# Spacing the feed-forward blocks of a macaron layer along a planner's beats

## The chip, the cores and the metric

The kernel runs on one core of a Trainium2 chip (trn2). The metric is device time of one execution in microseconds (us), as the median of three runs. The five engines are called as in the profile: PE (TensorE matmuls; PEld are its weight loads), DVE (VectorE), ACT (ScalarE), POOL (GpSimd) and SP (SyncE, which only issues DMAs here).

## The reference

32 sequences of 256 tokens with 128 features pass through one "macaron" layer: half a feed-forward block, attention, half a feed-forward block.

```python
x = x + 0.5 * ffn(layernorm(x))        # first FFN
x = x + attn(layernorm(x))             # 16 heads of 8, softmax, then a layernorm of (ctx + input)
x = x + 0.5 * ffn(layernorm(x))        # second FFN, same weights

def ffn(x):                            # weights are +1 or -1, drawn as booleans
    h = concat([x, -x])
    h = s0 * (h @ k0);  h = relu(h) * 2     # 512 features
    h = s1 * (h @ k1);  h = relu(h) * 2     # 512
    return s2 * (h @ k2)                    # 128
```

## The kernel before

Two sequences make a unit of 512 tokens; there are 16 units (`NU`). For each unit the kernel does a first FFN (`first`), a normalization and projection for attention (`norm_attn`, `project`), row maxima of the scores (`maxima`), a shift row made from them (`shift`), the softmax weights and their products with the values (`weigh`), the context with its layernorm (`context`), and a second FFN (`second`). Activations that feed a matmul are held as a sum of a high and a low fp16 part, so each 512-column product of an FFN is two passes on PE.

An FFN of a unit is 4 steps of layer 0 and 16 steps of layer 1 (two passes of 128x512 each) and 4 groups of layer 2 (8 passes of 128 columns). After each 128x512 result `relu_split` makes the high part on ACT (L663) and the low part on DVE (L664). The planner may move that work: the low part to POOL, after a full-precision copy on ACT (L666, then L661), or both parts to POOL (L667, then L661). The last sum can go from DVE (L718) to ACT and POOL (L719, L720) in the same way.

`maxima` and `weigh` set the beat. Each of a unit's 16 beats has one score tile for the maxima (`nat`, L825, reduced on DVE at L836 into `nm`) and, 13 beats later (`BW`), one for the weights (`sc`, L895, exponentiated on ACT at L907 into `pt`). Both kinds take the same pool of two PSUM tiles. Products with the values (`cx`, L877) follow each pair of `sc` tiles. There are 256 beats of maxima; the beats of weights end 13 later.

All operations go into a list with an engine, an assumed cost and a *rank*, which is a place on the scale of beats. `_Plan.simulate` runs through that list at build time with the assumed costs, and so decides which instruction is emitted next on each engine: on PE the lowest ranks first, with FFN work (kind "F") used as filling between the beats; on the others the lowest rank that is ready. The order found is fixed; on the chip each engine runs its own queue in that order and waits on semaphores. The constants at the top (`BIAS`, `CAST`, `SKIP`, `RUSH`, `AHEAD` and others) steer this planner and do no work of their own.

A matmul can be emitted in two tilings: dense ("D", L420, one 128x128 weight) or as four column tiles ("C", L423, four of 128x32). Score tiles use row tiles of 32 ("R"). The planner takes for an FFN step the tiling that PE is in.

Where an FFN's work lies along the beats is set by its rank:

```python
first(u):   rank = B0 + P0 * u                 # B0 = -30, P0 = 16.003
second(u):  rank = B1 + max(u * UNIT, P1 * min(u, SLOW) + P2 * max(u - SLOW, 0))
            # UNIT = 16, B1 = 42.462, P1 = 17.354, SLOW = 1, P2 = 16
```

so both kinds follow each other at 16 beats, one of each per unit. `QF` and `QK` say for how many units the normalizations take a quick form, which is done on DVE (L612) in place of POOL (L617, L618).

Of the kernel before, what the change touches and what calls it, by code (L numbers as in the profile page):

```python
# [41 lines left out]
ALU = mybir.AluOpType  # L42
# [7 lines left out]
EPS = 1e-5  # L50
# [4 lines left out]

PT, NXN = 5, 5

QF, QK = 1, 1

QL = 1  # L60

# [1 line left out]


UNIT = 16
B0, BA, BP, BW, BV, B1 = -30, -10.627, -6.547, 13, 4, 42.462

P0, P1, P2, SLOW = 16.003, 17.354, 16, 1

TURN_X, TURN_C = 1.5, 1.5  # L70

WARM = 14

BB = 15.813

RUSH, AHEAD = -0.12, 4.08

SKIP0, SKIP, UNTIL = 10.311, 2.868, 28.215

FAR = 19.64  # L80

HOLD = (0, 0.0, 0.0)

CAST = 1.0

WAIT = 0.057

KIND2 = 'F'

# [2 lines left out]

AFTER, REACH = (0.165, 0.085, 0.11, 0.04, 0.0), (0.053, 0.033, 0.037, 0.08, 0.05)

BIAS = 1.115

BIAS2 = 0.714
PE, DVE, ACT, POOL, SP = range(5)


# [19 lines left out]
class _Plan:  # L120
# [11 lines left out]
    def op(self, eng, cost, emit, r=(), w=(), rank=0.0, kind="D", rows=0, lag=None, alt=None, rush=False):  # L132
        x = _Node()
        x.n, x.eng, x.cost, x.emit, x.rank, x.kind, x.rows = len(self.nodes), eng, cost, emit, rank, kind, rows
        x.lag, x.alt, x.tiling = lag, alt, "D"
        x.then, x.avail, x.start, x.rush = [], 0.0, None, rush
        x.pair = None
        needs = set()
        for k in r:
            if k in self.wrote:  # L140
                needs.add(self.wrote[k])
        for k in w:
            if k in self.wrote:
                needs.add(self.wrote[k])
            needs.update(self.read.pop(k, ()))
        for k in r:
            self.read.setdefault(k, []).append(x)
        for k in w:
            self.wrote[k] = x
        needs.discard(x)  # L150
        x.needs = list(needs)
        for y in x.needs:
            y.then.append(x)
        x.bufs = []
        for k in (*r, *w):
            b = k[0] if isinstance(k, tuple) else k
            if isinstance(b, _Buf) and b not in x.bufs:
                x.bufs.append(b)
                b.left += 1
        self.nodes.append(x)  # L160
        return x
# [228 lines left out]
def tile_macaron(ctx: ExitStack, tc: tile.TileContext, x, Wq, bq, Wk, bk, Wv, bv, gamma, beta, k0, k1, k2, s0, s1, s2, out):  # L390
    nc = tc.nc
    plan = _Plan(tc)
    op = plan.op
# [3 lines left out]
    NU = B // 2  # L397
    TU = 2 * S
    NT = TU // P
# [94 lines left out]
    scale = const.tile([P, 3], F32, name="scale")  # L494
# [5 lines left out]
    def projections():  # L500
# [15 lines left out]
        s = lambda emit, w, rank=-700: op(SP, 0.42, emit, w=w, rank=rank, lag=4.5)  # L516
        v = lambda cost, emit, r, w, rank=B0 + BB: op(DVE, cost, emit, r=r, w=w, rank=rank)
        for i, (W, b) in enumerate(((Wq, bq), (Wk, bk), (Wv, bv))):
# [71 lines left out]
    def normalize(dst, src, tag, n, rank, scale=1.0, quick=False):  # L590

        of = lambda: src[0].t[:, src[1] : src[1] + n]
        srcs = [(src[0], src[1] + t) for t in range(0, n, 2)]
        mv = buf(small, [P, n, 2], F32, f"mv{tag}", 4, f"mv_{tag}")
        ve = buf(small, [P, n], F32, f"ve{tag}", 4, f"ve_{tag}")
        rs = buf(small, [P, n, 1], F32, f"rs{tag}", 4, f"rs_{tag}")
        step = 2 if quick else n
        for a in range(0, n, step):
            part = slice(a, a + step)
            ts = range(a, a + step)  # L600
            for t in ts:
                st = buf(small, [P, 6], F32, f"st{tag}", 4, f"st_{tag}_{t}")
                op(DVE, 0.195, lambda t=t, st=st: nc.vector.bn_stats(st.t, of()[:, t, :]), r=[srcs[t // 2]], w=[st], rank=rank)
                op(DVE, 0.085, lambda t=t, st=st: nc.vector.bn_aggr(mv.t[:, t, :], st.t), r=[st], w=[(mv, t)], rank=rank)
            op(POOL, 0.27, lambda part=part: nc.gpsimd.tensor_scalar(ve.t[:, part], mv.t[:, part, 1], EPS, 1.0 / scale**2, ALU.add, ALU.mult),
               r=[(mv, t) for t in ts], w=[(ve, a)], rank=rank)
            op(POOL, 0.35 + 0.2 * step, lambda part=part: nc.gpsimd.tensor_tensor(rs.t[:, part, 0], ve.t[:, part], nhalf[:, part], ALU.pow),
               r=[(ve, a), "nhalf"], w=[(rs, a)], rank=rank)
        mvs = [(mv, t) for t in range(n)]
        if quick:  # L610
            for t in range(n):
                op(DVE, 0.26, lambda t=t: nc.vector.tensor_scalar(dst.t[:, t, :], of()[:, t, :], mv.t[:, t, 0:1], rs.t[:, t, :], ALU.subtract, ALU.mult),  # L612
                   r=[srcs[t // 2], (rs, t // 2 * 2), (mv, t)], w=[(dst, t)], rank=rank)
        else:
            dsts = [(dst, t) for t in range(n)]
            cost = 0.2 + 0.2 * n
            op(POOL, cost, lambda: nc.gpsimd.tensor_tensor(dst.t, of(), bc(mv.t[:, :, 0:1], D), ALU.subtract), r=[*srcs, *mvs], w=dsts, rank=rank)  # L617
            op(POOL, cost, lambda: nc.gpsimd.tensor_tensor(dst.t, dst.t, bc(rs.t, D), ALU.mult), r=[(rs, 0)], w=dsts, rank=rank)  # L618
# [19 lines left out]
    xs, xns, xTs, nms, cxs = {}, {}, {}, {}, {}  # L638
# [11 lines left out]
    def norm_ffn(key, src, n, rank, quick):  # L650
        name = f"{key[0][-1]}_{key[1]}_{key[-1]}"
        xn = buf(work, [P, n, D], F32, "fxn", 2, f"fxn{name}")
        normalize(xn, src, f"f{key[0][-1]}", n, rank, XS, quick)
        xTs[key] = turned(xn, key[0][-1], name, n, rank)
# [15 lines left out]
    def ffn(key, srcs, n, rank, span):  # L670

        xT = xTs.pop(key)
        w = n * P
        name = f"{key[0][-1]}_{key[1]}_{key[-1]}"

        at = lambda i: rank + span * i / (NF + NF * NF + n)
        LAYER2 = (lambda k: k) if KIND2 == "F" else (lambda k: 2 * (k // 2) + 0.9)
        i = 0
        h1 = [buf(work, [P, NF, w], F16, f"h1{p}", 2, f"h1{p}{name}") for p in "hl"]
        h2 = [buf(work, [P, NF, w], F16, f"h2{p}", 2, f"h2{p}{name}") for p in "hl"]  # L680
        step = 2 * w / 2370
        for m in range(NF):
            ph = psum([P, w], f"p1{name}_{m}")

            def layer0(tiling, m=m, ph=ph):
                for k in range(2):
                    dense(ph.t, w0[:, bass.ts(m, P)], xT.t[:, k, :], tiling, k == 0, k == 1)

            op(PE, step, layer0, r=["w0", *((xT, i, a) for i in range(2) for a in range(0, n, 2))], w=[ph], rank=at(i), kind="F")
            relu_split(*h1, m, ph, w, at(i))  # L690
            i += 1
        for m in range(NF):
            ph = psum([P, w], f"p2{name}_{m}")
            for c in range(NF):

                def layer1(tiling, m=m, c=c, ph=ph):
                    for k in range(2):
                        dense(ph.t, w1[:, c, bass.ts(m, P)], h1[k].t[:, c, :], tiling, c == 0 and k == 0, c == NF - 1 and k == 1)

                op(PE, step, layer1, r=[("w1", c), (h1[0], c), (h1[1], c)], w=[ph], rank=at(i), kind="F")  # L700
                i += 1
            relu_split(*h2, m, ph, w, at(i))
        po = psum([P, n, D], f"p3{name}")
        h2s = [(h, m) for h in h2 for m in range(NF)]
        for t in range(n):

            def layer2(tiling, t=t):
                for c in range(NF):
                    for k in range(2):
                        dense(po.t[:, t, :], h2[k].t[:, c, bass.ts(t, P)], w2[:, c, :], tiling, c == 0 and k == 0, c == NF - 1 and k == 1)  # L710

            op(PE, 0.449, layer2, r=[*h2s, "w2"], w=[po], rank=LAYER2(at(i)), kind=KIND2)
            i += 1
        src, part = srcs
        full = buf(work, [P, w], F32, "full", 2, "full")
        to = lambda: src.t[:, part : part + n]
        dsts = [(src, part + t) for t in range(0, n, 2)]
        op(DVE, 0.08 + w / 870, lambda: nc.vector.scalar_tensor_tensor(to(), po.t, fac, to(), ALU.mult, ALU.add), r=[po, "fac"], w=dsts, rank=at(i),  # L718
           alt=(0.09 + w / 1040, lambda: nc.scalar.activation(full.t.rearrange("p (t d) -> p t d", d=D), po.t, AF.Identity, scale=fac), po, full,  # L719
                0.1 + w / 455, lambda: nc.gpsimd.tensor_tensor(to(), to(), full.t.rearrange("p (t d) -> p t d", d=D), ALU.add)))  # L720
        return dsts

    def norm_first(u):
        norm_ffn(("ffn0", u), (xs[u], 0), NT, (B0 + P0 * u - AHEAD) if u >= QF else B0 - 0.5 + 2 * (u - 1) if u else -950, u < QF)

    def first(u):
        rank = B0 + P0 * u
        ffn(("ffn0", u), (xs[u], 0), NT, rank, P0)

    def second(u, b):  # L730
        n, part = (NT, 0) if b is None else (2, 2 * b)
# [270 lines left out]
```

## Time and profile before

| | us |
|---|---|
| median of 3 runs | 688.27 (687.88 to 688.88) |
| time of the profiled execution | 689.46 |
| its span, first to last instruction | 687.6 |
| PE busy | 659.8 (96%) |
| DVE busy | 581.1 (85%) |
| ACT busy | 543.1 (79%) |
| POOL busy | 497.3 (72%) |
| granted TensorE clock, mean | 0.995 |

Matmuls are pipelined and their ends are modelled, so a busy PE is not a PE at its peak; the distance from the start of one matmul to the start of the next tells what it costs. A line of a table by stretch of time reads: the stretch, its length, then for each engine the busy time with the number of instructions in brackets, then the granted TensorE clock, the share of DMA engines busy and GB/s. A chain of waits reads: start, length, what the end of the kernel was waiting for at that time. An execution in the profile is 1.2 us slower than the median of the runs; differences are made inside the profiled execution and then taken to the median.

### The profile page before, as it was taken

What the parts mean: (1) busy time and instruction counts of PE and PEld (TensorE: products, weight loads), DVE (VectorE), ACT (ScalarE), POOL (GpSimd) and SP (SyncE); (2) the same over time, 40 slices, a digit from 0 to 9 for tenths busy, and PEclk for the clock granted to TensorE, in tenths of its full rate; (3) what the DMA queues carried; (4) which work ended last, traced back from release to release, by engine and by line L of the source; (5) the groups of instructions that cost most, each with busy time, mean ns of one, the idle gap of its engine ahead of it and who ended that gap; (6) DMA issues with size and microseconds to landing.
All of it is one profiled execution on the core that took longest, in us unless ns stands there. A gap on an engine that the chain in (4) does not pass through costs nothing.

```text
span 687.6 us, 28926 instructions
## 1 busy us (share of the span) xinstructions
PE 659.8 (96%) x12596; PEld 344.6 (50%) x12596; DVE 581.1 (85%) x1194; ACT 543.1 (79%) x871; POOL 497.3 (72%) x685
## 2 busy tenths in 40 slices
PE   7998978999999999999999999999999999999996
PEld 4544533545455554555455454555445454544455
DVE  7789887998989798898979889897988888889484
ACT  3546887788889888888978888897889787868953
POOL 6875596688686868768686877868686785865643
PEclk9999998999999999999999999999999999999999
DMA  7222200203011030301102030200203021300000
GB/s 222 76 79 80 64 23 3 83 5 98 5 49 54 3 98 4 100 4 58 46 5 97 3 99 5 76 27 16 86 5 97 4 74 30 96 4 20 5 17 31
DMA packets 33391, 33.59 MB, mean 49 GB/s; under 512 B 4992, under 2 KB 29056, under 8 KB 33264
## 3 DMA queue, kind: packets, MB, share of 16 engines
q1 hardware_dynamic: 31520, 30.89, 14.3%
q8 instruction: 99, 1.62, 1.0%
q10 hardware_dynamic: 1744, 0.85, 0.4%
q14 instruction: 28, 0.23, 0.1%
HBM read 18.58 MB, written 13.14 MB: 46 GB/s over the span
## 4 chain that ended last, share of the span: by engine, by line
PE 82%; DVE 7%; ACT 4%; POOL 3%; DMA 2%; issue 1%; SPq 0%; ACTq 0%; POOLq 0%
PE p_None L423 18%; PE p L423 17%; PE cx L877 16%; PE sc L895 9%; PE p L420 6%; DVE nm L836 4%; PE p_None L420 3%; PE nat L825 3%; ACT pt L907 2%; PE tp L921 2%; PE pq L423 2%; PE pq L420 1%; PE pv L423 1%; PE t L630 1%; PE t_None L630 1%
## 5 line engine op out<-in xcount | busy, mean ns | idle before, releaser
L836 DVE TENSOR_REDUCE nm<-nat 128x4 f32<-128x1024 f32 x256 | 310.5, 1216 | 27.4 <-PE nat L825 22.0
L907 ACT ACTIVATE pt<-sc,esc 128x1024 f32<-128x1024 f32 x256 | 285.2, 1116 | 54.7 <-PE nat L825 45.2
L423 PEld LDWEIGHTS <-w 128*32 128x32 f16 x3976 | 97.4, 96 | 102.4 <-issue 28.9
L877 PE MATMUL cx<-pt,vaug 128*32 128x256 f32 x2048 | 137.2, 385 | 0.0
L895 PE MATMUL sc<-qs,ks 32*128 32x256 f16 x1024 | 103.2, 274 | 6.7 <-ACT pt L907 4.9
L825 PE MATMUL nat<-ks,qs 32*128 32x256 f16 x1024 | 101.7, 274 | 3.9 <-ACT pt L907 1.8
L877 PEld LDWEIGHTS cx<-pt,vaug 128*32 128x32 f32 x2048 | 58.6, 110 | 44.7 <-issue 12.3
L423 PE MATMUL p<-h1h,w 128*32 128x512 f16 x796 | 78.5, 383 | 0.0
L423 PE MATMUL p<-h1l,w 128*32 128x512 f16 x796 | 78.0, 380 | 0.0
L423 PE MATMUL p_None<-h1h_None,w 128*32 128x512 f16 x744 | 73.6, 382 | 0.1
L423 PE MATMUL p_None<-h1l_None,w 128*32 128x512 f16 x744 | 73.0, 379 | 0.0
L895 PEld LDWEIGHTS <-ks 32*128 32x128 f16 x1024 | 31.7, 92 | 75.0 <-issue 70.7
L661 POOL TENSOR_TENSOR h2l_None<-full,h2h_None 128x512 f16<-128x512 f32 x27 | 31.5, 1168 | 27.6 <-ACT full L666 27.3
L661 POOL TENSOR_TENSOR h2l<-full,h2h 128x512 f16<-128x512 f32 (+1 forms) x36 | 40.8, 1134 | 11.5 <-ACT full L666 10.8
L663 ACT ACTIVATE h1h<-p 128x512 f16<-128x512 f32 (+1 forms) x68 | 37.3, 577 | 13.6 <-PE p L420 9.0
L825 PEld LDWEIGHTS <-qs 32*128 32x128 f16 x1024 | 31.3, 92 | 29.7 <-issue 28.7
L663 ACT ACTIVATE h2h<-p 128x512 f16<-128x512 f32 (+1 forms) x56 | 32.3, 576 | 15.7 <-PE p L420 11.8
L664 DVE SCALAR_TENSOR_TENSOR h2l_None<-p_None,h2h_None 128x512 f16<-128x512 f32 x33 | 22.7, 687 | 25.7 <-ACT h2h_None L663 25.6
L420 PEld LDWEIGHTS <-w 128*128 128x128 f16 x326 | 30.1, 98 | 28.5 <-issue 10.5
L664 DVE SCALAR_TENSOR_TENSOR h1l<-p,h1h 128x512 f16<-128x512 f32 (+1 forms) x61 | 39.4, 663 | 1.1 <-ACT h1h L663 0.8
L663 ACT ACTIVATE h2h_None<-p_None 128x512 f16<-128x512 f32 x56 | 33.4, 596 | 6.0 <-PE p_None L420 4.9
L423 PE MATMUL p_None<-xT_None,w 128*32 128x512 f16 x480 | 35.4, 380 | 0.0
(163 smaller groups left out, 1471.7 us busy)
## 6 DMA issues: line engine op xcount, KB each, us to landing
dr<-qkhl SPq DMA_DIRECT2D x32, 256.0 KB, 2.0
qs<-dr SPq DMA_DIRECT2D x48, 128.0 KB, 3.3
ks<-dr SPq DMA_DIRECT2D x48, 128.0 KB, 2.6
out_dram<-x SPq DMA_DIRECT2D x15, 256.0 KB, 3.0
x<-in_L_attn_x_dram SPq DMA_DIRECT2D x14, 256.0 KB, 6.1
dm<-mr SPq DMA_DIRECT2D x32, 16.0 KB, 2.5
qs<-dm SPq DMA_DIRECT2D x32, 16.0 KB
qs<-nought SPq DMA_DIRECT2D x13, 32.0 KB
```

The lines of the kernel that those rows point to most:

```text
L420: nc.tensor.matmul(to, w, of, start=start, stop=stop)
L423: nc.tensor.matmul(to[32 * r : 32 * r + 32], w[:, 32 * r : 32 * r + 32], of, start=start, stop=stop)
L630: nc.tensor.transpose(pt.t[:, bass.ts(t, P)], xn.t[:, t, :], ident)
L661: return lambda: nc.gpsimd.tensor_tensor(lo.t[:, m, :], of.t, hi.t[:, m, :], ALU.subtract)
L663: h = op(ACT, 0.09 + w / 1280, lambda: nc.scalar.activation(hi.t[:, m, :], ps.t, AF.Relu), r=[ps], w=[(hi, m)], rank=rank)
L664: l = op(DVE, 0.08 + w / 985, lambda: nc.vector.scalar_tensor_tensor(lo.t[:, m, :], ps.t, 0.0, hi.t[:, m, :], ALU.max, ALU.subtract), r=[p ...
L825: nc.tensor.matmul(nat.t[:, ii, qc, :], Q[32 * r : 32 * r + 32, g, b * S + qc * P : b * S + qc * P + P], K[32 * r : 32 * r + 32, g, b * S ...
L836: op(DVE, 1.141, lambda g=g, pr=pr, nat=nat: nc.vector.tensor_reduce(nm.t[:, :, 2 * pr : 2 * pr + 2, g].rearrange("p q i -> p i q"), nat.t ...
L877: nc.tensor.matmul(cx.t[32 * r : 32 * r + 32, g // 2, :], V[:, 2 * b + kc, 4 * (g // 2) + r, 16 * (g % 2) : 16 * (g % 2) + 32], pts[g, r / ...
L895: nc.tensor.matmul(sc.t[:, ii, kc, :], K[32 * r : 32 * r + 32, g, b * S + kc * P : b * S + kc * P + P], Q[32 * r : 32 * r + 32, g, b * S : ...
L907: op(ACT, 1.012, lambda pt=pt, sc=sc: nc.scalar.activation(pt.t, sc.t, AF.Exp, scale=esc), r=[sc, "esc"], w=[pt], rank=rank - RUSH, rush=True)
L921: nc.tensor.transpose(tp.t[:, qc, 8 * c : 8 * c + 8, :].rearrange("p h n -> p (h n)"), cxT.t[:, c, bass.ts(qc, P)], ident)
```

## The change

First FFNs are no longer 16 beats apart. The new function `place0` puts those of units 0 to 6 12 beats apart and the later ones 18.67 apart, so that the last one keeps its place (beat 210). Second FFNs are 16.95 beats apart up to unit 10 and 13.42 apart after it, but never before beat `B1 + 16 u`. The quick normalizations cover more units at the start, and the planner's other constants get other values, among them the assumed cost of a cast on POOL (`CAST`, 1.0 to 0.62). No operation of the layer is added or removed.

```diff
-QF, QK = 1, 1
+QF, QK = 3, 2
-B0, BA, BP, BW, BV, B1 = -30, -10.627, -6.547, 13, 4, 42.462
-P0, P1, P2, SLOW = 16.003, 17.354, 16, 1
-TURN_X, TURN_C = 1.5, 1.5
+B0, BA, BP, BW, BV, B1 = -30, -11.429, -5.976, 13, 4, 44.465
+P1, P2, SLOW = 16.954, 13.418, 10
+EARLY, COUNT, OVER = 12, 6, 0
+TURN_X, TURN_C = 0.3, 1.5
-BB = 15.813
-RUSH, AHEAD = -0.12, 4.08
-SKIP0, SKIP, UNTIL = 10.311, 2.868, 28.215
+BB = 10.463
+RUSH, AHEAD = 0.144, 4.667
+SKIP0, SKIP, UNTIL = 7.606, 3.049, 23.783
-CAST = 1.0
-WAIT = 0.057
+CAST = 0.62
+WAIT = 0.125
-BIAS = 1.115
-BIAS2 = 0.714
+BIAS = 1.03
+BIAS2 = 0.765
...
-            op(POOL, 0.27, lambda part=part: nc.gpsimd.tensor_scalar(ve.t[:, part], ...
+            op(POOL, 0.275, lambda part=part: nc.gpsimd.tensor_scalar(ve.t[:, part], ...
...
+    def place0(u):
+        rest = ((NU - 1) * UNIT + OVER - EARLY * COUNT) / (NU - 1 - COUNT)
+        return B0 + EARLY * min(u, COUNT) + rest * max(u - COUNT, 0)
+
     def norm_first(u):
-        norm_ffn(("ffn0", u), (xs[u], 0), NT, (B0 + P0 * u - AHEAD) if u >= QF else B0 - 0.5 + 2 * (u - 1) if u else -950, u < QF)
+        norm_ffn(("ffn0", u), (xs[u], 0), NT, place0(u) - AHEAD if u >= QF else B0 - 0.5 + 2 * (u - 1) if u else -950, u < QF)
     def first(u):
-        rank = B0 + P0 * u
-        ffn(("ffn0", u), (xs[u], 0), NT, rank, P0)
+        ffn(("ffn0", u), (xs[u], 0), NT, place0(u), min(UNIT, place0(u + 1) - place0(u)))
```

More of the change, by code (lines that the diff above doesn't have):

```diff
@@ L604, in normalize @@
                 op(DVE, 0.085, lambda t=t, st=st: nc.vector.bn_aggr(mv.t[:, t, :], st.t), r=[st], w=[(mv, t)], rank=rank)
-            op(POOL, 0.27, lambda part=part: nc.gpsimd.tensor_scalar(ve.t[:, part], mv.t[:, part, 1], EPS, 1.0 / scale**2, ALU.add, ALU.mult),
+            op(POOL, 0.275, lambda part=part: nc.gpsimd.tensor_scalar(ve.t[:, part], mv.t[:, part, 1], EPS, 1.0 / scale**2, ALU.add, ALU.mult),
                r=[(mv, t) for t in ts], w=[(ve, a)], rank=rank)
```

## The prediction

> **What bounds the kernel now.** I read the page's slices first, then the time and the beats in six stretches (a beat is one `nat` tile of four matmuls), then the chain of waits in the middle and near the end, then PE's timeline for what a matmul costs.
>
> ```profile
> PE   7998978999999999999999999999999999999996
> PEclk9999998999999999999999999999999999999999
> ```
>
> PE has holes in the first ten slices and in the last; one slice early on has a lower clock. By stretch:
>
> ```profile
> core 0: us, PE busy (x) PEld busy (x) DVE busy (x) ACT busy (x) POOL busy (x), PEclk, DMA share, GB/s
> 0.00:43.15 43.15, 36.60 (x230) 21.41 (x231) 32.62 (x111) 21.34 (x48) 32.20 (x51) 1.00 0.50 149
> 43.15:66.90 23.75, 21.26 (x431) 10.19 (x431) 23.30 (x34) 13.59 (x26) 14.26 (x17) 1.00 0.19 59
> 66.90:155.70 88.80, 81.68 (x1517) 40.22 (x1520) 78.00 (x154) 70.59 (x106) 66.19 (x92) 0.96 0.12 35
> 155.70:574.20 418.50, 418.19 (x8672) 217.88 (x8671) 363.96 (x729) 356.67 (x566) 316.29 (x425) 1.00 0.15 47
> 574.20:638.80 64.60, 60.24 (x1152) 29.61 (x1144) 56.95 (x100) 51.24 (x73) 45.90 (x67) 1.00 0.11 33
> 638.80:687.60 48.80, 41.87 (x612) 25.27 (x608) 26.28 (x69) 29.62 (x53) 22.42 (x36) 0.99 0.06 19
> ```
>
> The cuts are at beats 0, 16, 56, 224 and 256: the same stretches asked for `nat` alone hold 0, 64, 162, 672, 128 and 0 matmuls (162 for 160 since a cut fell inside a tile). A beat takes 88.80/40 = 2.22 us, then 418.50/168 = 2.49, then 64.60/32 = 2.02. In the middle PE has no hole, and the chain shows the same step of PE every unit:
>
> ```profile
> 248.98 1.29 PE p_None L423 x24
> 288.65 1.29 PE p_None L423 x24
> 328.33 1.29 PE p_None L423 x24
> ```
>
> 39.67 us a unit: there PE is the bound. Near the end a beat is cheaper in PE work, and the chain leaves PE:
>
> ```profile
> 612.61 1.11 ACT pt L907
> 613.72 0.50 ACT h2h_None L663
> 614.24 0.69 DVE h2l_None L664
> 614.93 1.14 DVE nm L836
> 616.12 0.26 PE nat L825
> 616.61 1.12 ACT pt L907
> ```
>
> Two beats here take 4.0 us: `pt`, a ReLU split queued behind it on ACT, its low part on DVE, the maxima behind that, then the next score tiles. This alternation over the two shared PSUM tiles, not PE, keeps such beats at 2 us.
>
> What PE work costs, from starts in the middle:
>
> ```profile
> 245.44 0.28 PE L895 MATMUL sc<-qs,ks 32*128 32x256 f16 x1
> 245.76 0.62 PE L423 MATMUL p_None<-xT_None,w 128*32 128x512 f16 x8
> 246.21 0.39 PE L423 MATMUL p<-h1h,w 128*32 128x512 f16 x4
> 246.42 0.39 PE L423 MATMUL p<-h1l,w 128*32 128x512 f16 x4
> 246.64 0.61 PE L423 MATMUL p_None<-xT_None,w 128*32 128x512 f16 x8
> ```
>
> A pass of 512 columns is 0.216 us (246.42 to 246.64), dense or in column tiles alike. A score pair with the change to row tiles is 0.32 us (245.44 to 245.76), of which 0.11 is the change of tiling: the same 0.11 stands before row tiles after column tiles (a group of `pv`, 12 passes of 0.056 us, starts at 242.05 and the scores after it at 242.84, not 242.72). So an FFN is 40 x 0.216 + 32 x 0.056 = 10.4 us of PE.
>
> **The change, part by part.** I took the order in which the instructions of both kernels stand on PE and gave each its duration (512 columns 0.216, 128 columns 0.056, `cx` of 8 matmuls 0.87, score pair 0.22, transpose 0.11, change of tiling 0.11). PE work in us, cut at the same beats:
>
> - before beat 0: 33.5 before, 38.7 after
> - beats 0 to 16: 20.0, 23.6
> - 16 to 56: 75.9, 82.5
> - 56 to 224: 414.9, 393.1
> - 224 to 256: 56.7, 63.0
> - the rest: 38.6, 40.1
>
> The sums, 639.6 and 641.0, agree but for changes of tiling: 573 before, 584 after, 11 x 0.11 = 1.2 us more. The middle loses 21.8 us; 15.4 go ahead of it (one and a half FFNs) and 7.8 behind it. The gain is what the edges swallow.
>
> *Before beat 0: +4.0.* PE runs with nearly no hole from 12.26 us to the first `nat` at 43.17; its holes there are 0.30, 0.30, 0.55, 0.52 and 0.45, together 2.1 us. Ahead of the first `nat` stand 22 more passes of 512 columns (4.75 us) and one more transpose group (0.44); the projection that feeds the first keys comes later too, behind most of them, so DMA and landing shift along. Filling half the holes leaves 5.2 - 1.1, about 4.0. Bounds 3 and 5.5. The quicker normalizations add 12 L612 instructions of 0.30 us to DVE, which has 10 us free here, and take 3 x 2.1 us of L617 and L618 from POOL.
>
> *Beats 0 to 16: +1.0.* DVE is busy 23.30 of 23.75, so DVE bounds. Its work in these beats grows by 0.5 us in the new order, and PE at 23.6 gets no slack. Bounds 0.5 and 3.
>
> *Beats 16 to 56: +1.2.* PE has 88.8 - 75.9 = 12.9 us over its work; 6.6 are filled. DVE's work stays at 78 us. The beats lengthen where the filling brings a split into the alternation shown, and against that stands the clock:
>
> ```profile
> 100.00:105.00 5.00, 3.39 (x42) 1.24 (x43) 3.50 (x8) 3.07 (x6) 4.52 (x10) 0.83 0.03 8
> 105.00:110.00 5.00, 3.86 (x40) 1.29 (x39) 3.01 (x6) 2.54 (x3) 2.47 (x4) 0.50 0.01 3
> ```
>
> After two slices with PE at 3.4 to 4 of 5 us the granted clock falls to half for some 6.8 us. PE is busy three quarters of that, so it loses 6.8 x 0.5 x 0.77 = 2.6 us at most. The Trainium skill ("TensorE: Matmul & The Clock Gate", Part 1, the warm-up mystery) puts the cold state after at least one idle window of about 3.4 us. The longest hole before the drop here is 1.2 us (at 93.6), so the row shows the fall under thinner PE work than the rule needs. By the rule a denser PE does nothing for the clock and this stretch costs +3.8; by the row the denser beats (14.7 and 14.4 us of work where 10.4 and 12.0 were) keep the clock up and it costs +1.2. I take the row. Bounds -1 and +6.6 (all new work added, none hidden).
>
> *Beats 56 to 224: -18.8.* The measured 418.5 is 3.6 over its work. The new work is 393.1; with the same 3.6 it is 396.7. The old order repeats unit by unit; the new one doesn't, so the other engines' loads shift against PE's. For what that costs the trace has one near row, the end of the repeating part: beats 192 to 224 (`nat` starts at 493.2 and 574.2) took 81.0 us for 79.8 of PE work, 1.2 over, where 32 repeating beats are 0.6 over. That is 0.02 us a beat, or 3 us over 168: 399.7, or 2.38 us a beat. Bounds 396.7 and, at three times that row, 405.7. Other engines allow it: DVE's work in these beats stays about 2.1 us a beat (88%, as 364/418.5 = 87% before), ACT about 2.0. POOL gets 17 more L661 (1.16 us) and 33 more L667 casts (0.61), in return for 6 L720 and the normalizations: +28 us in the whole kernel, from 76% to some 85% here. ACT loses 16 of L666 (0.60 us), DVE 17 of L664 (0.69) and gains 6 of L718 and 12 of L612. None of these is on the path while PE has work; that cover is thinnest for POOL.
>
> The skill's rule against the change: "TensorEngine Tiling (Array Packing)", Tiling Modes, says that a change of tiling mode drains TensorE. The row prices that drain at 0.11 us, and all 11 more are in the sums; priced by the rule alone no figure would follow.
>
> *Beats 224 to 256: +4.0.* PE has 7.9 us over its work and 6.3 are to be filled, 4.0 of them into the first eight beats (15.8 to 19.8 us of work, measured 16.9). Those eight become PE-bound at about 20.0; the other 24 stay on the 2 us alternation (48.6 us for the 47.7 measured). Half an FFN brings four splits of 0.50 + 0.69 = 4.8 us if all are on the chain. Bounds 2 and 6.3.
>
> *The rest: +1.0.* Of the second FFN of unit 13, 26 passes are left after the last `nat`, before 20: 1.3 us, in beats that ACT's exponentials hold (5.87 of 6.20 us busy after 638.8). Behind the last context two passes more: 0.4. Bounds 0 and 2.
>
> SP issues the same transfers in nearly the same order. Loads of x were all issued at the start, and stores follow their second FFN: no cost, with PE work as cover.
>
> Sum: 4.0 + 1.0 + 1.2 - 18.8 + 4.0 + 1.0 = -7.6. The profiled execution took 689.46, so 681.9 for it; the median lies 1.2 under that, so 680.7, rounded to 681.
>
> **The rivals.** *Ragged middle, slower (chance 0.14).* Without the old period a beat of the middle waits for POOL's low parts or for DVE before PE can go on. It decides at 2.38 + 7.6/168 = 2.425 us a beat; beyond, the kernel is slower. For it: beats 16 to 56, also irregular, carry 12.9/40 = 0.32 us of PE idle each, and POOL rises to 85%. Against: there PE had too little filling, and 192 to 224, with enough, lost 1.2/32 = 0.04. At 0.08 over my forecast the kernel takes 681 + 0.08 x 168 = 694.
>
> *The edges swallow little (chance 0.14).* Early and late beats lengthen by all their new work: 5.2 + 3.6 + 6.6 + 6.3 + 1.5 = 23.2 against -18.8: +4.4, 693. For it: DVE at 98% in beats 0 to 16, the alternation near the end. Against: over 12 us of PE idle lie in beats 16 to 56 with the same DVE load. Half of this, 687, is a likelier form, still faster; so a third of this chance ends faster and some of it level.
>
> *The edges swallow nearly all (chance 0.12).* Clock kept, early beats no longer than now, middle at 396.7: 3.0 + 0.5 - 1 - 21.8 + 2 + 0 = -17 at most; half way to that is 676.
>
> That the change doesn't do what it says is excluded: in PE's new order the first FFN of unit 2 is nearly done before the first `nat`, where before it had just begun.
>
> **How the numbers follow.** Forecast 0.60 (681, own range 676 to 686), ragged 0.14, little swallowed 0.14, nearly all 0.12. Faster by over 0.2% (1.4 us, about what a measurement of this kernel can tell from no change): 0.60 + 0.12 + 0.05 (edges by half) + 0.02 (a slightly ragged middle) = 0.79; within 0.2%: 0.03 + 0.02 of the two slower rivals = 0.05; slower: 0.06 + 0.10 = 0.16. The range goes from 675, under which half of "nearly all" lies, to 689.5, above which most of the slower cases lie.
>
> **What would show it.** First `nat` at about 47 us, beat 56 near 162, beat 224 near 562, beat 256 near 630; no clock drop near 105; a middle beat at 2.38 us with PE without holes; late beats at 2.1 us. If a middle beat is over 2.42, or the chain there leaves PE for POOL h1l, h2l or DVE nm, the forecast is wrong in the middle; if beat 56 is past 168, it is wrong in the early beats.

## The result, and the profile after

The changed kernel takes 693.04 us in the median (16 runs, 688.96 to 696.63) where the kernel before takes 688.04 beside it (16 runs, 687.15 to 689.96): ratio 1.0066, 95% interval 1.0049 to 1.0082. It is slower by two thirds of a per cent; the forecast was 681. Its profiled execution took 693.77 us, with a span of 692.0 (before: 689.46 and 687.6).

The slices of the page of the changed kernel, in the same columns as before:

```profile
PE   7899999999999999999999999999999999989997
PEclk9999999999999999999999999999999999999999
```

The holes of slices 4, 6 and 7 are gone, as the change says. But slice 2 is emptier than before (8 for 9), slice 36 has a hole now, and the whole is longer, so one has to look by stretch. The same stretches as in the prediction, cut at beats 0, 16, 56, 224 and 256 (stretch, length, busy time of PE, PEld, DVE, ACT, POOL with instruction counts, granted clock, DMA share, GB/s):

```profile
0.00:53.15 53.15, 44.34 (x256) 25.50 (x257) 39.50 (x132) 24.35 (x53) 39.74 (x65) 0.97 0.40 121
53.15:78.40 25.25, 24.39 (x563) 12.59 (x563) 24.14 (x40) 17.80 (x36) 20.46 (x23) 1.00 0.18 56
78.40:169.00 90.60, 85.66 (x1728) 42.77 (x1723) 78.24 (x159) 72.49 (x109) 76.64 (x106) 1.00 0.11 34
169.00:574.40 405.40, 400.81 (x8141) 202.99 (x8137) 353.29 (x689) 333.01 (x521) 314.47 (x432) 1.00 0.15 48
574.40:644.60 70.20, 66.28 (x1412) 34.00 (x1415) 59.85 (x106) 54.68 (x80) 49.95 (x71) 1.00 0.11 35
644.60:692.00 47.40, 42.66 (x618) 25.25 (x610) 26.80 (x73) 28.94 (x50) 21.75 (x36) 1.00 0.06 19
```

| stretch | before | after | difference | forecast |
|---|---|---|---|---|
| to beat 0 | 43.15 | 53.15 | +10.0 | +4.0 |
| beats 0 to 16 | 23.75 | 25.25 | +1.5 | +1.0 |
| 16 to 56 | 88.80 | 90.60 | +1.8 | +1.2 |
| 56 to 224 | 418.50 | 405.40 | -13.1 | -18.8 |
| 224 to 256 | 64.60 | 70.20 | +5.6 | +4.0 |
| the rest | 48.80 | 47.40 | -1.4 | +1.0 |
| sum | 687.6 | 692.0 | +4.4 | -7.6 |

Two terms carry the whole miss: 6.0 us at the start and 5.7 in the middle. Without one of them the kernel would still have been faster or level; with both it is slower.

**The start.** The timeline from 18 us on shows three engines in one knot. First POOL (start, length, operation), which never pauses:

```profile
18.36 1.39 POOL L578 MEMSET vaug<- 128x1536 f32 x1
19.72 1.18 POOL L663 TENSOR_TENSOR h2l<-full,h2h 128x512 f16<-128x512 f32 x1
20.84 0.95 POOL L579 MEMSET ks<- 128x1024 int32 x1
21.73 0.95 POOL L586 MEMSET qs<- 128x1024 f32 x1
```

The group of DVE's quick normalizations between 17 and 24 us (shortest, median and longest in ns, first and last start):

```profile
L614 DVE TENSOR_SCALAR fxn<-x,mv_f,rs_f x6: 339/788/2939, 16.8 to 19.8; 128x128 f32<-128x128 f32 x6
```

And PE's timeline:

```profile
22.84 0.66 PE L632 MATMUL t<-ident,fxn 128*128 128x128 f32 x4 [3.35 <-DVE h2l L666]
```

An instruction that takes 0.34 us at best takes 2.94: it starts at 19.82 and ends at 22.76, when POOL's row of three instructions ends (21.73 + 0.95). The low part `h2l` stands behind it in DVE's queue, and PE has nothing left: a hole of 3.35 us. The next lines say what follows from it:

```profile
19.50:23.00 3.50, 0.16 (x1) 0.17 (x2) 3.34 (x8) 0.60 (x1) 3.18 (x4) 1.00 0.49 138
23.00:28.00 5.00, 4.95 (x18) 2.08 (x18) 2.04 (x7) 1.93 (x5) 1.92 (x3) 0.66 0.00 0
```

PE is busy 0.16 us of 3.50, and then the granted clock is 0.66 over 5 us: in the trace, half clock from 24.2 us for 3.4 us. Here the rule of the Trainium skill ("TensorE: Matmul & The Clock Gate", Part 1) of an idle window of some 3.4 us fits the hole of 3.35 us; shorter holes in the runs below had half clock behind them in some executions and not in others.

**The middle.** PE's idle time in beats 56 to 224 was 418.50 - 418.19 = 0.31 us before and is 405.40 - 400.81 = 4.6 us now. The waits of PE there, the four longest of seven in the changed kernel and then the only one in the kernel before (who, for whom: total us, times, longest):

```profile
PE p L425 <- issue: 1.2, 2, 1.1
PE pm L861 <- DVE h2l_None L666: 0.8, 1, 0.8
PE nat L831 <- ACT pt L913: 0.6, 1, 0.6
PE sc L901 <- DVE nm L842: 0.3, 1, 0.3
```

```profile
PE pq L423 <- DVE xTa L634: 0.2, 1, 0.2
```

The four waits have four different causes. `h2l` is no input of `pm`, nor `pt` one of `nat`: there PE waits for a PSUM tile that they read. The counted PE work in these beats is 393.1 us, so the stretch is 12.3 us over its work, where it was 3.6 over before; the other part of the excess must lie inside PE's busy time, since the ends of matmuls are modelled and short stalls don't show as holes.

### The profile page after: what moved, and what is told of

Same layout as the page of the kernel before. It is cut to its first block, busy times and chain, and to the rows that moved or that the text cites. A ratio compares the mean times of both kernels' runs of the same rounds, so it can differ in the third digit from the quotient of the medians.

```text
span 692.0 us, 29141 instructions
## 1 busy us (share of the span) xinstructions
PE 664.1 (96%) x12695; PEld 343.1 (50%) x12695; DVE 581.8 (84%) x1195; ACT 531.3 (77%) x849; POOL 523.0 (76%) x729
## 4 chain that ended last, share of the span: by engine, by line
PE 81%; DVE 8%; ACT 6%; issue 2%; DMA 1%; POOL 1%; SPq 0%; ACTq 0%; POOLq 0%; DVEq 0%
PE p_None L425 18%; PE cx L883 15%; PE p L425 14%; PE sc L901 9%; PE p L422 7%; PE p_None L422 5%; DVE nm L842 3%; ACT pt L913 3%; PE nat L831 2%; PE tp L927 2%; PE pq L425 2%; PE ta L632 1%; PE t L632 1%; PE t_None L632 1%; PE pv L425 1%
## 5 line engine op out<-in xcount | busy, mean ns | idle before, releaser
L425 PEld LDWEIGHTS <-w 128*32 128x32 f16 x3464 | 84.1, 96 | 85.9 <-issue 30.3
L425 PE MATMUL p<-h1l,w 128*32 128x512 f16 x660 | 65.2, 379 | 1.1 <-issue 1.1
L425 PE MATMUL p<-h1h,w 128*32 128x512 f16 x660 | 65.6, 383 | 0.2 <-DVE h1l L666 0.2
L422 PEld LDWEIGHTS <-w 128*128 128x128 f16 x454 | 43.1, 99 | 39.4 <-issue 9.9
L422 PE MATMUL p<-h1h,w 128*128 128x512 f16 (+1 forms) x123 | 42.2, 355 | 1.3 <-DVE h1l L666 0.9
L422 PE MATMUL p<-h1l,w 128*128 128x512 f16 (+1 forms) x123 | 42.3, 357 | 0.0
L663 POOL TENSOR_TENSOR h2l<-full,h2h 128x512 f16<-128x512 f32 (+1 forms) x30 | 33.9, 1129 | 5.1 <-ACT full L668 4.1
L605 DVE BATCH_NORM_STATS2 st_f<-x 128x6 f32<-128x128 f32 x128 | 31.3, 274 | 7.4 <-POOL x L947 4.8
L663 POOL TENSOR_TENSOR h1l<-full,h1h 128x512 f16<-128x512 f32 (+1 forms) x30 | 33.4, 1114 | 2.7 <-ACT full L668 1.9
L665 ACT ACTIVATE h1h<-p 128x512 f16<-128x512 f32 (+1 forms) x55 | 31.5, 579 | 5.1 <-PE p L422 3.2
```

The lines of the kernel that those rows point to most:

```text
L422: nc.tensor.matmul(to, w, of, start=start, stop=stop)
L425: nc.tensor.matmul(to[32 * r : 32 * r + 32], w[:, 32 * r : 32 * r + 32], of, start=start, stop=stop)
L663: return lambda: nc.gpsimd.tensor_tensor(lo.t[:, m, :], of.t, hi.t[:, m, :], ALU.subtract)
L665: h = op(ACT, 0.09 + w / 1280, lambda: nc.scalar.activation(hi.t[:, m, :], ps.t, AF.Relu), r=[ps], w=[(hi, m)], rank=rank)
```

## The experiments

In what follows, times by stretch are read at the first `nat` of beats 0, 16, 56 and 224, and "over its work" is a stretch's time less PE's work counted from the order. e1, e2 and e4 to e8 start from the changed kernel, e3 and e13 from the kernel before, e9 to e12 and e14 from e5. e6 to e9 and e13 leave out work of the layer and e14 does some twice, so their medians are no times of the whole layer.

| run | to beat 0 | 0 to 16 | 16 to 56 | 56 to 224 | over its work | after 224 | median | ratio to before (95%) |
|---|---|---|---|---|---|---|---|---|
| before | 43.2 | 23.7 | 88.8 | 418.6 | 3.7 | 113.3 | 688.04 | |
| after | 53.2 | 25.2 | 90.6 | 405.3 | 12.3 | 117.6 | 693.04 | 1.0066 (1.0049 to 1.0082) |
| e1 no quick | 49.6 | 27.5 | 90.7 | 405.6 | 12.5 | 117.8 | 693.22 | 1.0076 (1.0061 to 1.0091) |
| e2 other form | 51.8 | 25.2 | 90.8 | 405.2 | 12.1 | 117.3 | 691.41 | 1.0044 (1.0028 to 1.0060) |
| e3 spacing alone | 50.8 | 28.2 | 92.1 | 416.4 | 23.2 | 120.2 | 710.28 | 1.0331 (1.0306 to 1.0355) |
| e4 constants alone | 51.8 | 23.7 | 95.5 | 426.3 | 9.9 | 111.5 | 710.85 | 1.0329 (1.0312 to 1.0346) |
| e5 port free | 49.0 | 25.2 | 91.0 | 405.4 | 12.4 | 117.2 | 689.09 | 1.0010 (1.0002 to 1.0019) |
| e6 light DVE | 50.2 | 25.2 | 90.6 | 403.4 | 10.3 | 117.4 | 690.80 | 1.0037 (1.0028 to 1.0046) |
| e7 light ACT | 52.1 | 25.2 | 90.5 | 404.3 | 11.2 | 116.9 | 691.61 | 1.0046 (1.0030 to 1.0062) |
| e8 light POOL | 51.1 | 25.2 | 90.5 | 405.5 | 12.4 | 116.8 | 691.62 | 1.0047 (1.0029 to 1.0064) |
| e9 short drains | 49.2 | 25.2 | 89.5 | 404.5 | 11.4 | 116.4 | 686.80 | 0.9973 (0.9960 to 0.9986) |
| e10 full span | 49.6 | 25.2 | 90.9 | 411.1 | 17.0 | 119.3 | 697.10 | 1.0119 (1.0095 to 1.0142) |
| e11 constants a | 50.3 | 26.3 | 90.8 | 403.7 | 10.9 | 118.2 | 692.56 | 1.0061 (1.0044 to 1.0078) |
| e12 constants b | 49.2 | 26.9 | 88.7 | 403.2 | 11.3 | 116.2 | 686.42 | 0.9966 (0.9953 to 0.9979) |
| e13 before, thin | 43.0 | 23.7 | 85.9 | 410.3 | 15.7 | 112.8 | 678.98 | 0.9856 (0.9839 to 0.9873) |
| e14 thick | 48.7 | 25.2 | 95.3 | 426.3 | 12.1 | 119.9 | 717.98 | 1.0423 (1.0402 to 1.0445) |

**The start: the quick normalizations, and the port.**

e1 takes the quick forms out of the changed kernel:

```diff
-QF, QK = 3, 2
+QF, QK = 1, 1
```

> The changed kernel with QF and QK back at 1: the normalizations of units 1 and 2 are done on POOL again, the spacing stays. Theory (DVE's quick normalizations are held up by POOL's memsets at 18 to 23 us, which opens the 3.35 us hole of PE and the 3.4 us at half clock after it): the first nat comes at 47 to 49 us in place of 53.2, no half clock between 20 and 40 us, and the time is 4 to 6 us under the changed kernel's, 687 to 689. Rival (the 22 more passes and the projection placed behind them delay the first nat, whatever does the normalization): first nat at 52 us or later, time within 1.5 us of the changed kernel's.

The first `nat` comes 3.6 us earlier and there is no half clock at the start, but beats 0 to 16 take 2.3 us more, and the total is the same, 4 us over what the theory had said. The quick normalizations are worth having, only not in this form, as e5 shows below.

e2 keeps their place and gives them a form with two tensors as input, in place of a scalar pointer (operands shortened):

```diff
-nc.vector.tensor_scalar(dst, x, mv, rs, ALU.subtract, ALU.mult)
+nc.vector.scalar_tensor_tensor(dst, x, mv, rs.broadcast_to([P, D]), ALU.subtract, ALU.mult)
```

> The changed kernel in the same order on all engines; only the form of the quick normalization on DVE differs: scalar_tensor_tensor with the reciprocal root broadcast along the row as a second tensor, in place of tensor_scalar with two pointer scalars. Theory (the tensor_scalar form takes the SBUF port that POOL's memsets hold; a form with two SBUF tensors meets a memset without waiting): no fxn on DVE between 17 and 23 us takes over 0.6 us, PE's hole of 3.35 us shrinks to under 1, no half clock at 24 us, first nat at 48 to 49.5 us, time 4 to 5 us under the changed kernel's. Rival (DVE waits there for the reciprocal roots from POOL, which is simply late): the hole stays at 3 us or more, time within 1 us of the changed kernel's.

In DVE's timeline of e2 (first fence; PE's is the second) two of them together take 0.60 us now; but another small instruction is caught a few us later, and PE behind it:

```profile
18.28 0.60 DVE L614 SCALAR_TENSOR_TENSOR fxn<-x,mv_f,rs_f 128x128 f32<-128x128 f32 x2
...
23.54 3.09 DVE L545 TENSOR_SCALAR diag<-ident,top 3x3 f32<-3x3 f32 x1
```

```profile
26.69 0.38 PE L546 MATMUL sp<-diag,ones 3*128 3x3 f32 x2 [1.90 <-DVE h1l L666]
```

Nine elements take 3.09 us: POOL's row of `vaug`, a cast, `ks` and `h1l` runs from 22.68 to 26.6 there. The hold-up had moved, not gone, and so had the half clock (27.0 us, behind a hole of only 1.90 us).

e5 gives `diag` two tensors as input too:

```diff
-nc.vector.tensor_scalar(diag, ident[0:3, 0:3], top[:, 3:4], None, ALU.mult)
+nc.vector.tensor_tensor(diag, ident[0:3, 0:3], top[:, 3:4].broadcast_to([3, 3]), ALU.mult)
```

> The changed kernel in the same order, with the quick normalization as scalar_tensor_tensor as in the run before and the 3x3 diagonal (L545) as a product with a broadcast second tensor in place of a pointer scalar, so that no SBUF-to-SBUF tensor_scalar meets POOL's memsets in the first 30 us. Theory (the hold-up moves to the next DVE instruction of that form; with both gone the start follows the plan): no DVE instruction under a running stretch of POOL takes over 0.8 us, no half clock before the first nat, first nat at 47.5 to 49.5 us where the changed kernel had 53.2, time 687 to 689. Rival (whatever leaves the start sooner waits in beats 0 to 16, as with the normalizations back on POOL, where 3.6 us gained before the first nat left 1.3 at beat 16): first nat at 49 us, but beat 16 at 76 us or later and time 690 to 692.

```profile
23.74 0.15 DVE L545 TENSOR_TENSOR diag<-ident,top 3x3 f32<-3x3 f32 x1
```

By stretch, over the same microseconds as for the changed kernel:

```profile
19.50:23.00 3.50, 3.27 (x17) 1.65 (x18) 2.56 (x9) 1.64 (x5) 3.50 (x6) 1.00 0.36 106
23.00:28.00 5.00, 4.67 (x49) 3.46 (x48) 4.72 (x12) 3.60 (x8) 4.30 (x7) 1.00 0.01 3
```

PE is busy 3.27 us of the 3.50 where it was 0.16, at full clock after it, although POOL is still busy all the time. Beat 0 comes 4.2 us earlier than in the changed kernel, and this time nothing is given back: the ratio falls from 1.0066 to 1.0010, 3.9 us. The order on every engine is that of the changed kernel. So the form of a few small DVE instructions is worth 4 us here, and the first half of the miss is settled. The medians say the same as the two profiles: of the changed kernel's 16 runs 10 show a mean clock of 0.998 or less and take 693.6 us on average, the 6 others 691.0; of e5's 20 runs none is under 0.999. The Trainium skill ("SBUF — State Buffer", Who interferes with whom) has DVE and GpSimd share one pair of ports under an exclusive lock, with the loser blocked for the whole of an instruction, and a DVE instruction with two SBUF inputs concerned only against one of GpSimd that reads SBUF; the memsets don't. e5's `diag` agrees (0.15 us under a memset), and the changed kernel and e2 add that the loser waited for a whole row of POOL's instructions, not for one. The new form isn't free of POOL either. In e5 the first two normalizations together take 1.34 us, while POOL's `h1l`, which reads SBUF, runs until 14.88 us. In e12 (below) the same `diag` takes 1.08 us and ends with a cast of POOL at 24.7 us, though it began 0.46 us before that cast, under a memset; this the rule doesn't explain.

**The two halves of the change.** e3 is the kernel before with the new spacing alone, e4 the changed kernel with the old spacing, so with the new constants alone (in short form):

```diff
 # e3, on the kernel before
-B1 = 42.462;  P0, P1, P2, SLOW = 16.003, 17.354, 16, 1
+B1 = 44.465;  P1, P2, SLOW = 16.954, 13.418, 10;  EARLY, COUNT, OVER = 12, 6, 0
-rank = B0 + P0 * u
+rank = place0(u)
 # e4, on the changed kernel: the reverse
```

> The kernel before with the new places of first and second FFNs alone (place0, P1, P2, SLOW, B1); QF, QK and all planner constants as before. Theory (places that are no multiple of the beats' period break the repeating order, and PE then waits for DVE and ACT in single beats): beats 56 to 224 take 8 us or more over their PE work, as the changed kernel's 12.3, where before had 3.7; the start is not late (first nat 43 to 47 us); time 684 to 690. Rival (the other constants, the cheaper cast above all, made the middle ragged): at most 5 us over the PE work in the middle, time 679 to 683.

> The changed kernel with the old places of both kinds of FFN (16 beats apart, B1 42.462); QF, QK and all other constants new. Theory (the raggedness comes from the places, the late start from the quick normalizations): the middle repeats again unit by unit, at most 5 us over its PE work; first nat at 48 us or later; time 691 to 698, no better than the changed kernel. Rival (the constants made the middle ragged): 8 us or more over the PE work in the middle, time 697 or more.

Both take some 22 us more than the kernel before: e3 more than either of its ranges, e4 within its rival's alone. With the constants of before the new spacing is 23.2 us over its work in the middle, as the theory of e3 had it; with the new constants the old spacing is 9.9 over, as the rival of e4 had it. So either half alone lengthens the middle over its work, and the effect of the change isn't a sum of parts. That the planner's constants are fitted to one spacing would explain it, but is argued, not shown.

e3's start adds something. Its quick normalizations are those of the kernel before, and still the first `nat` is 7.6 us later: `diag` (L545) waits 3.87 us, from 21.71 on, through four POOL instructions that end at 25.55, PE has a hole of 2.24 us, and half clock sets in at 25.4 us for 3.4. So what holds DVE up isn't bound to the quick normalizations; it depends on where POOL's row meets a DVE instruction of this form.

**The middle: load of an engine.** Three kernels keep the changed kernel's order and take away work of one engine in units 4 to 13 (in short form):

```diff
 # e6: maxima over half of the keys          # e7: exponentials of half of a tile
-nm <- max(nat.t)                            -pt.t <- exp(sc.t)
+nm <- max(nat.t[:, :, :, 0 : S // 2])       +pt.t[:, :, :, 0 : S // 2] <- exp(sc.t[:, :, :, 0 : S // 2])
 # e8: POOL's low parts over half of the columns
-lo.t[:, m, :] <- of.t - hi.t[:, m, :]
+lo.t[:, m, 0:k] <- of.t[:, 0:k] - hi.t[:, m, 0:k]     # k = w // 2
```

> The changed kernel in the same order; in units 4 to 13 the maxima on DVE are taken over half of the keys (half of the row is left out, and the exponent's scale is a sixteenth so that nothing overflows), 0.5 us less of DVE in each of 160 beats. The middle (beats 56 to 224) took 405.3 us for 393.1 of PE work in the changed kernel. If PE waits there for DVE, or for the maxima in the alternation over the two score tiles: at most 398 us. If it waits for ACT or POOL: 402 or more.

> The changed kernel in the same order; in units 4 to 13 the exponentials on ACT are made for half of each score tile (the other half is left out, the products with the values read the first half twice), 0.5 us less of ACT in each of 160 beats. If PE waits for ACT in the middle: at most 398 us for beats 56 to 224. If it waits for DVE or POOL: 402 or more.

> The changed kernel in the same order; in units 4 to 13 the low parts that POOL makes after a copy on ACT are made for half of the columns (the rest is left out, and PE reads the first half twice), 0.5 us less for each of some 70 such instructions. If PE waits for POOL in the middle, as the rival of a ragged middle had it: at most 399 us for beats 56 to 224. If it waits for DVE or ACT: 403 or more.

DVE does 79 us less in the middle, ACT 55 and POOL 21, and the middle gains 1.9, 1.0 and nothing. None of the three engines alone holds it up. (The starts of these runs and of the changed kernel lie between 50.2 and 53.2 us with one order. The last two quick normalizations take 4.10 us together in the changed kernel and in e7, with a PE hole of 3.35 us and half clock behind it; in e6 and e8 they take 2.32, with holes of 2.15 and 1.90 us and no half clock. So the 4.2 us are what the hold-up cost in one execution; the medians' 3.9 are the firmer number.)

**The middle: PSUM tiles, gaps between FFNs, the constants.** e9 halves the columns that ACT and DVE read of a hidden layer's PSUM tile, and POOL of ACT's copy; e10 spreads each FFN's 24 pieces up to the next of its kind; e11 and e12 shift the planner's constants and keep the spacing.

In short form:

```diff
 # e9, units 4 to 13, every form of the split       # e10
-relu(ps.t); ps.t - hi                              -span = min(UNIT, at(u + 1) - at(u))
+relu(ps.t[:, 0:k]); ps.t[:, 0:k] - hi[:, 0:k]      +span = at(u + 1) - at(u)      # and for first() likewise
```

> e5 with the same order on every engine, but in units 4 to 13 every evacuation of a hidden layer (the ACT relu L665, the DVE low part L666 and their POOL forms) takes half of the columns; left out: the other half of the hidden layer, whose matmuls read the first half twice, so PE's instructions are the same. The PSUM tile of a hidden layer is read for about half as long, and so given back sooner. Theory (the three PSUM tiles that all FFN pieces, projections and turns share, 'm', come back too late in the beats in which the FFNs' phases fall badly; the trace of after shows pm L861 idle 0.79 us behind the DVE read h2l, which is no input of it): the middle, beats 56 to 224, falls from 405.4 to 399 or less, the total to 684 or less. Rival one (engine load alone; the three runs that lightened DVE, ACT and POOL one at a time gained 2.0, 1.1 and -0.1 us in the middle): about 402.5. Rival two (beats without filling between two FFNs of a kind, where no ready piece exists): 404 to 406.

> e5 with each FFN's ten pieces spread over the whole distance to the next FFN of its kind (18.7 and 17.0 beats in the middle) instead of over at most 16 beats, so that no beats are left between two FFNs of one kind. Rival two of the run beside it (the 2.7 and 1.0 beats without filling between FFNs of a kind are what costs the middle): the middle falls from 405.4 to 399 or less. Theory (PSUM tiles held too long): the accumulating tiles are held over more beats, so the middle is no shorter, 404 to 412, and the total 688 to 697.

> e5 with small shifts of its constants, the spacing kept (BA -11.342, BB 10.75, RUSH 0.057, SKIP0 8.352, UNTIL 22.4, CAST 0.496, WAIT 0.136, TURN_C 1.362): a new order with the same filling per beat on average. If the excess of the middle is that of drifting phases, which any order of this spacing has somewhere, the middle stays 402 to 407 and the total 686 to 691, but the late beats are other ones. If it was bad luck of one order, the middle is 396 to 400 and the total 680 to 684, which would beat both kernels.

> As the run before, with other small shifts (B0 -30.013, OVER 0.213, AHEAD 4.861, SKIP 3.033, TURN_C 1.026, CAST 0.618, BIAS 0.997). Drifting phases: the middle 402 to 407, the total 686 to 691, late beats again in other places. Bad luck of one order: 396 to 400 and 680 to 684.

e9: 404.5 in the middle, so the PSUM theory, mine at that point, fell; of the 2.9 us by which its span is shorter, 0.9 lie in the middle. e10: 411.1, so filling the beats between two FFNs doesn't help, and spreading further is worse; but that is a new order, with accumulating tiles held over more beats, so it doesn't exclude that those beats cost something. e11 and e12: 403.7 and 403.2. With the constants of the changed kernel or near them, every order at this spacing that does the whole work lies 10.9 to 12.5 us over it in the middle (e10 17.0), with PE idle for 3.9 to 5.0 us (e10 8.7). A hole of 0.6 to 0.7 us behind ACT's `pt` at beat 79 is in each of them but e10; most of the others move, and stand behind other engines. The total of e11 missed its own range by 1.6 us, for its edges are longer.

e12 beats both kernels: 686.42 us, 0.34% under the one before. It gains 2.3 us in beats 16 to 56 and 2.2 in the middle over e5, and gives back 1.7 in beats 0 to 16.

**The middle: how much filling, or in what order.** e13 leaves six of the forty 512-column passes of each FFN out of the repeating order of before; e14 does seven of them twice in the order of e5:

```diff
 # e13, layer 1 in units 4 to 13
-for k in range(2):
+for k in (0,) if cut and (c == 1 or c == 2 and m < 2) else (0, 1):
 # e14
+for k in (0, 1, 1) if cut and (c == 1 or c == 2 and m < 3) else (0, 1):
```

> The kernel before with thinner filling in its repeating order: in units 4 to 13 six of the forty 512-column passes of each FFN are left out (low parts of the second layer), nothing else, so the order on every engine and the work of DVE, ACT and POOL are those of before. PE's work in beats 56 to 224, counted from the order, falls from 414.9 to 394.6 us, 2.35 us a beat, which is what the changed kernel has (393.1). Theory one (the middle of the changed kernel is long because its order doesn't repeat with the unit): the repeating order stays about 4 us over its work, middle 397 to 400, PE still without holes. Theory two (thin filling: at 2.35 us of PE work a beat the other engines' alternation ends some beats, in whatever order): 10 to 13 us over its work, middle 404 to 408.

> The reverse on e5: in units 4 to 13 seven passes of each FFN are done twice, so that PE's work in beats 56 to 224 rises from 393.1 to 414.2 us, 2.47 us a beat, as in the kernel before, in the order of the changed one. Theory one (no repetition): the middle stays about 12 us over its work, 425 to 428. Theory two (thin filling): the thicker beats cover the other engines, about 4 to 6 us over, middle 418 to 420.

The middle of e13, then of e14:

```profile
152.60:562.90 410.30, 403.64 (x8317) 208.77 (x8316) 362.38 (x730) 356.07 (x567) 316.91 (x427) 1.00 0.15 48
```

```profile
169.20:595.50 426.30, 421.61 (x8455) 213.40 (x8448) 356.08 (x690) 334.59 (x521) 314.94 (x433) 1.00 0.15 45
```

In the old order 20.3 us less PE work (394.6 in place of 414.9) bring only 8.3: PE, idle 0.31 us before, is idle 6.7 us in it now, and the stretch is 15.7 over its work, more than theory two had said. Its chain of waits shows what lay underneath. Of these 410 us the chain stands for 247 on PE, for 86 on ACT and for 65 on DVE; in the kernel before all but 2 us of the middle stood on PE. Two pieces of it:

```profile
330.57 0.63 DVE x L719
331.21 0.09 DVE mv_c L604
331.30 1.11 DVE nm L837
...
339.82 1.11 ACT pt L908
340.94 0.50 ACT h2h_None L663
341.46 0.70 DVE h2l_None L664
```

First it is DVE's queue, without a pause, then the same alternation of ACT and DVE that the prediction saw in the late beats. In the changed order the outcome is theory one's: 21.1 us more PE work cost 20.9, and the 12.1 over its work stay (1.0 us of them a new hole of PE behind a DMA of `ks`); thicker filling covers next to nothing there. And its chain (e5) hardly leaves PE: 382 of 405 us. So each order has its own reason: the old one is short of cover as soon as PE's work shrinks, and the new one has places where PE waits whatever the filling weighs. One limit: e13 keeps an order that was planned for the fuller work, and no run plans it anew for the thinner.

## Why the prediction was wrong

*Before beat 0 (+4.0; measured +10.0).* The step that failed is the one that gave the quick normalizations to "DVE, which has 10 us free here", at no cost. Free time of an engine isn't enough: one takes 0.34 us at best, and up to 2.94 in a row of POOL's instructions. e5 shows 4.2 us of the 10.0 to be this (the PE hole and the half clock after it). The other 5.8 is the new work of 5.2 with none of PE's small holes filled (from 12.3 us on they come to 2.3 us in e5, for 2.1 before), where I had half of them filled: a little over the upper bound of 5.5.

*Beats 0 to 16 (+1.0; +1.5)* and *224 to 256 (+4.0; +5.6)* were within their bounds. *The rest (+1.0; -1.4)* was not: its bounds were 0 and 2, and no run says why it got shorter. The edges apart from the start took 7.5 us for a forecast of 7.2, a sum in which these errors cancel, so its closeness is luck. With the start they took 17.5 of the 23.2 us of new work, where 11.2 were forecast: about half of the rival that they swallow little came, and most of that half by the hold-up at the start, which it doesn't name.

*Beats 16 to 56 (+1.2; +1.8).* There is no clock drop near 105 us, but the reason was weaker than I made it. Of 42 runs of the kernel before on one chip, 34 show a mean clock of 0.998 or more, and take 688.1 us on average; 8 show less, and take 689.7. The drop in the profiled execution is one of the few, worth some 1.6 us. Against an execution without it the stretch costs about 1.8 + 1.6 = 3.4 us, an estimate from these figures, which is near the +3.8 that I gave for no help from the clock. That +1.8 lies near +1.2 is owed to the execution that was profiled. The row that I set against the rule was a row of one execution (e4 has another such drop, at 96.2 us with no hole over 0.9 us in the 10 us before it); and having counted a gain from it, I took off another 1.2 us on the way from that execution to the median, though most runs don't have the drop.

*Beats 56 to 224 (-18.8; -13.1).* The step that failed is "with the same 3.6", and the 3 us beside it for the raggedness. Both carry an excess over from an order in which PE hides everything else. e13 measures that this excess is no constant: with the changed kernel's amount of filling the old order itself is 15.7 us over. A PE without holes says that PE is the bound, and nothing of how far below the next bound lies; for the old order it lay at 2.44 us a beat (410.3/168), 0.05 under the 2.49 of before, and the forecast went to 2.38. The changed order got to 2.41, better than the thinned old one, so 2.44 is a bound of that one order and not of the engines. In place of 3.6 + 3 the changed order measured 12.3 us over its work.

*The rival "ragged middle"* named the right place and most of the signs (waits for DVE, holes where there were none). It was to decide at 2.425 us a beat, with every other term at its forecast; the beat came out at 2.413, and the start did the rest. Of the signs that would show a wrong forecast, beat 56 past 168 us came (169.0), and 6.0 of its 7 us are the start's. POOL, the engine I thought thinnest, was at 314.47/405.40 = 78%, not 85%, and e8 shows that it wasn't a bound.

Open: what in the changed order makes the waits of the middle. Shown is that lightening DVE, ACT, POOL or the PSUM reads one at a time doesn't take them away, that thicker filling doesn't, and that other constants move most of them and take away at most 1.5 us of the excess. e9 shortens only the reading of the tiles, and e10 changes the order besides, so PSUM and the beats without filling are not excluded as a part of it. That such an order doesn't repeat with the unit, so that the constants can't be fitted to one pattern of 16 beats, is argued, not shown. Nor does the trace say what PE waits for in the holes named "issue" (1.07 us at 423.05).

## What to carry to other kernels

When work is taken away from a bound engine, the saving ends at the next bound: measure that one by thinning the work in the same order before counting on the rest, and remember that another order may have its next bound elsewhere. Before giving small DVE instructions with a pointer scalar to a place where POOL has a row of memsets and copies, look at what POOL does in those microseconds, or give them two tensors as input. Take a clock drop for a property of a kernel only when more than one execution shows it.

## What the runs showed of the hardware

A DVE `tensor_scalar` from SBUF to SBUF waited through a row of three POOL instructions, 2.94 us in place of 0.34, and one of 3x3 elements took 3.09 us (e2) and 3.87 us (e3) in place of 0.22 (the kernel before). With `scalar_tensor_tensor` and `tensor_tensor` on two SBUF tensors the same work in the same place took 0.60 us for two and 0.15 (e5), but the latter 1.08 in e12.

With a PE hole of 3.35 us came 3.4 us of half clock (the changed kernel, e7), and so it did with one of 2.24 us (e3) and one of 1.90 us (e2), but not with one of 2.15 us (e6) or one of 1.90 us (e8). In the profiled execution of the kernel before, with PE busy 3.2 to 4.0 us of each 5 and no hole over 1.2 us, the clock fell to half for 6.8 us at 103.3 us; of 42 runs of that kernel 8 show a mean clock under 0.998.
